# Stationary operands of the second attention product: even and odd columns in place of the two halves, and one product group in reverse order

## The chip, the cores and the metric

The kernel runs on one core of one Trainium2 chip. The metric is the device time of one execution in microseconds. The kernel before takes 2455.51 us, the median of three runs (2453.16 to 2455.78). The profile was taken of another execution, of 2453.05 us, whose instructions span 2451.3 us. TensorE (PE in the profile) was granted 0.999 of its full clock in it.

## What is computed

The reference is one self-attention layer on an input x of 4 images of 64 x 64 pixels with 256 channels, in float32:

```
q = einsum('bwhc,cd->bwhd', x, Wq) + bq        # 128 channels
k = einsum('bwhc,cd->bwhd', x, Wk) + bk        # 128 channels
v = einsum('bwhc,cd->bwhd', x, Wv) + bv        # 256 channels
pq, pk, pv = q.reshape(B, -1, N), k.reshape(B, -1, N), v.reshape(B, -1, N)   # N = 64 * 64
energy = einsum('bcn,bcm->bnm', pq, pk)
attention = softmax(energy, axis=-1)
out = einsum('bcm,bnm->bcn', pv, attention)
return gamma * out.reshape(x.shape) + x
```

For each of the 4 images this is an N x N = 4096 x 4096 matrix of energies, its softmax over m, and a product of that matrix with the 256 channels of v. The reshape is a reinterpretation of memory, so a row of pq is a run of pixels and channels and not one channel. The two large products dominate.

## The kernel before

**Tiling.** An image is worked through in 16 groups of 256 columns n (`NG`, index `g`), and a group in 8 steps of 512 rows m (`NU`, index `t`). With 4 images there are 4 x 16 x 8 = 512 steps, counted within an image by `u`. A step has two halves on TensorE:

- `energy` (L317 on) forms the energies of a later step (three ahead). It multiplies stationary blocks of k (128 x 128) with the moving operand q (128 x 256). Every operand is split into a high part, a low part and a correction, so that products in the fast format fp32r give full precision; a step has 12 such products (L330), eight into the tile `sa` and four into `sb`.
- `attend` (L363 on) multiplies the exponentials with v. The exponentials of the step are held in three tiles: `h` (high part), `l` (the rest) and `d` (a correction), each of 128 partitions x 4 blocks of m x 256 columns n. They are the stationary operands, 128 columns at a time. The moving operands are rows of `vh`, `vl` (258 wide: 256 channels and two columns of ones that give the sum of the softmax) and `vd` (256 wide).

A step has 3 parts (`h`, `l`, `d`) x 2 blocks of columns (`j`) x 4 blocks of m (`i`) = 24 products in `attend` (L380), so 36 with the energies. Every product needs a fresh stationary operand: each MATMUL has a weight load of its own, which the profile lists as LDWEIGHTS under the engine name PEld.

**Blocks of columns.** Block `j` of the stationary operand is `left[:, i, j*P:(j+1)*P]`: 128 neighbouring float32 values, 512 bytes, with a step of 4 bytes. The rows of the accumulators `acc[j]` and `bb[:, j, :]` are the columns n of that block.

**Places in memory.** All of this lies in SBUF. Rows of `vh` and `vl` are 260 values (1040 bytes) apart, those of `vd` 256 values (1024 bytes). Blocks `i` of `h`, `l` and `d` are 1024 bytes apart. `l` and `d` have two buffers each and `h` has three, each 4096 bytes. Small unused tiles (`pad`, `pad2`, `pad3`) set where the tiles start.

**Order.** The order of the work is written out by hand (`manual_schedule`); each engine runs its list in order. In a step TensorE does the 12 energy products of step u + 3 and then the 24 of `attend(u)`: the eight of `h`, the eight of `l`, the eight of `d`, and within a part j = 0 and then j = 1, each with i = 0 to 3. ScalarE (ACT) does the exponentials (L334) and `h` (L349), VectorE (DVE) the join of two exponentials (L344) and `l` and `d` (L355, L358). At the end of a group, `finish` (L400 on) scales the sums, transposes them back through TensorE into `tp` (L417), and adds them to the tile `xr` of the input (L421), which goes out by DMA. The last group of all has its own form, `finish_last`, with the addition at L465.

Of the kernel before, what the change touches and what calls it, by code (L numbers as in the profile page):

```python
# [13 lines left out]
ALU = mybir.AluOpType  # L14
# [6 lines left out]
def kernel(  # L21
# [36 lines left out]
    nc = tc.nc  # L58
    B, W, H, C = x.shape
    P = 128  # L60
# [115 lines left out]
    NJ = NB // P  # L176
# [24 lines left out]
    with ExitStack() as fast:  # L201
# [161 lines left out]
        def attend(b, u):  # L363

            g, t = divmod(u, NU)
            if t == 0:
                now["acc"] = [
                    ps_o.tile([P, C + 2], F32, tag=f"a{j}", name=f"a{j}_{b}_{g}")
                    for j in range(NJ)
                ]  # L370
                now["bb"] = ps_o.tile([P, NJ, C], F32, tag="bb", name=f"bb_{b}_{g}")
            h, l, d = units[b, u]
            acc, bb = now["acc"], now["bb"]
            for left, right in ((h, vh), (l, vl), (d, vd)):
                for j in range(NJ):
                    out_ = bb[:, j, :] if left is d else acc[j]
                    for i in range(4):
                        m = 2 * t + i // 2 + NI * (i % 2)

                        nc.tensor.matmul(  # L380
                            out_,
                            left[:, i, j * P : (j + 1) * P],
                            right[:, m, : out_.shape[1]],
                            start=(t == i == 0 and (left is h or left is d and j == 0)),
                            stop=(t == NU - 1 and i == 3 and left is not h),
                            skip_group_check=True,
                        )
            if t == NU - 1 and (b, g) != (B - 1, NG - 1):
                o = now["o"] = work.tile([P, NJ, C + 2], F32, tag="o", name=f"o_{b}_{g}")
                for j in range(NJ):  # L390
                    nc.scalar.activation(o[:, j, :], acc[j], AF.Identity, scale=1.0 + E)

        def factors(b, g, gamma):

            r = work.tile([P, 2, NJ], F32, tag="r", name=f"r_{b}_{g}")
            nc.vector.reciprocal(r[:, 0, :], zall[:, b * NG + g, :])
            nc.vector.tensor_tensor(r[:, 0, :], r[:, 0, :], gamma.to_broadcast([P, NJ]), ALU.mult)
            return r[:, 0, :], r[:, 1, :]

        def finish(b, g, o, bb, xr):  # L400
            yield
            yield

            nc.vector.tensor_copy(zall[:, b * NG + g, :], o[:, :, C])
            r, _ = factors(b, g, gam1)
            nc.vector.tensor_tensor(o[:, :, :C], o[:, :, :C], bb, ALU.add)
            yield
            for j in range(NJ):
                nc.scalar.activation(
                    o[:, j, :C], o[:, j, :C], AF.Identity, scale=r[:, j : j + 1]  # L410
                )
            yield
            yield
            tp = ps_t.tile([P, 2, NB], F32, tag="t", name=f"ot_{b}_{g}")
            for s in range(2):
                for j in range(NJ):
                    nc.tensor.transpose(  # L417
                        tp[:, s, j * P : (j + 1) * P], o[:, j, s * P : (s + 1) * P], ident
                    )
            yield  # L420
            nc.vector.tensor_tensor(xr, xr, tp, ALU.add)  # L421
            nc.gpsimd.dma_start(ov[b, g], xr)

        def guard():

            z = zall.rearrange("p n j -> p (n j)")
            ok = ppool.tile([P, 4, NB], F32, tag="y", name="ok")[:, 0, : B * NG * NJ]
            nc.vector.tensor_scalar(ok, z, Z_LOW, None, ALU.is_ge)
            nc.vector.scalar_tensor_tensor(ok, z, Z_HIGH, ok, ALU.is_le, ALU.mult)
            yield  # L430
            nc.vector.tensor_reduce(zs, ok, AX.X, ALU.min)
            nc.vector.tensor_scalar(zs, zs, 0.5, None, ALU.is_lt)
            zp = ps_s.tile([P, 1], F32, tag="b", name="zp")
            nc.tensor.matmul(zp, ones, zs, start=True, stop=True)
            yield
            nc.vector.tensor_copy(again, zp)
            yield
            yield

        def finish_last(b, g, xr):  # L440

            for j in range(NJ):
                a = now["acc"][j]
                nc.vector.tensor_copy(zall[:, b * NG + g, j : j + 1], a[:, C : C + 1])
            r, ra = factors(b, g, gam)
            check = guard()
            nc.vector.tensor_scalar(ra, r, 1.0 + E, None, ALU.mult)
            o = work.tile([P, NJ, C + 2], F32, tag="o", name=f"o_{b}_{g}")
            tps = []
            for j in range(NJ):  # L450
                next(check)
                nc.scalar.activation(
                    o[:, j, :C], now["bb"][:, j, :], AF.Identity, scale=r[:, j : j + 1]
                )
                nc.vector.scalar_tensor_tensor(
                    o[:, j, :C], now["acc"][j][:, :C], ra[:, j : j + 1], o[:, j, :C], ALU.mult, ALU.add
                )
                tp = (ps_t, ps_s)[j].tile([P, 2, P], F32, tag="ta"[j], name=f"ot_{b}_{g}_{j}")
                for s in range(2):
                    nc.tensor.transpose(tp[:, s, :], o[:, j, s * P : (s + 1) * P], ident)  # L460
                tps.append(tp)
            for j in range(NJ):
                next(check)
                n = slice(j * P, (j + 1) * P)
                nc.vector.tensor_tensor(xr[:, :, n], xr[:, :, n], tps[j], ALU.add)  # L465
            nc.sync.dma_start(ov[b, g], xr)

        def begin(b, i):
# [17 lines left out]
        for b in range(B):  # L486
# [20 lines left out]
            for u in range(STEPS):  # L507
                g, t = divmod(u, NU)
# [33 lines left out]
                for forms in beside:  # L542
                    next(forms)
                attend(b, u)
                if (b, u) == (B - 1, STEPS - 1):
                    finish_last(b, g, loads.pop((b, "x", g)))
                elif t == NU - 1:
                    start(finish(b, g, now["o"], now["bb"], loads.pop((b, "x", g))))
# [9 lines left out]
    NJ = NB // P  # L558
    NP = NM // 2
    xg, og = columns(x, NB), columns(out, NB)  # L560
    with tc.If(nc.values_load(again[0:1, 0:1]) > 0), ExitStack() as general:
# [8 lines left out]
        for b in range(B):  # L570
# [16 lines left out]
            for g in range(NG):  # L587
                ps = []
                mx = work.tile([P, 2, NB], F32, tag="mx", name=f"gmx_{b}_{g}")
                for t in range(NP):  # L590
# [9 lines left out]
                    p = ppool.tile([P, 2, NB], F32, tag="p", name=f"gp_{b}_{g}_{t}")  # L600
# [6 lines left out]
                tp = ps_t.tile([P, NJ, P], F32, tag="t", name=f"gmt_{b}_{g}")  # L607
# [40 lines left out]
                xr = xpool.tile([P, 2, NB], F32, tag="xr", name=f"gxr_{b}_{g}")  # L648
# [41 lines left out]
```

## Time and profile before

| Part | Busy, us | Share of the span |
|---|---|---|
| TensorE matmuls (PE) | 2438.7 | 99% |
| TensorE weight loads (PEld) | 2408.0 | 98% |
| VectorE (DVE) | 2099.0 | 86% |
| ScalarE (ACT) | 1795.2 | 73% |
| GpSimd (POOL) | 424.5 | 17% |

Matmuls overlap each other in these records: one of 256 columns is shown as some 280 ns long, while the next one starts some 115 ns after it. The busy share of PE therefore says only that there was always a matmul in flight. What counts is the **pitch**, the time from the start of one matmul to the start of the next. It is read from the timeline: a row there merges a run of equal instructions and has the start of the first one, so the difference of two starts, divided by the number of products between them, is their pitch.

The DMA queues moved 204 GB/s on average, with a mean busy share of the DMA engines of 0.6 to 0.7 in most of the span.

### The profile page before, as it was taken

Reading aid. Unit: us, or ns where it says so; the run is one execution under the profiler, and the core shown is the slowest. Engines: PE = TensorE matmul, PEld = TensorE weight load, DVE = VectorE, ACT = ScalarE, POOL = GpSimd, SP = SyncE. Lnnn points to the kernel's source line nnn. Section 1 sums busy time; section 2 is a strip of 40 time slices with the busy share of each in tenths; the row PEclk is TensorE's granted clock in tenths of the full one; section 3 lists DMA queues with packets and bytes.
Section 4 is the critical chain, followed back from the end, with each engine's and each line's share of the span. In section 5 each row is a group of like instructions: output and inputs, shape, how many; then the busy total and the mean of one; then the engine's idle time right before and its main releaser. Section 6 shows DMA issues by size and latency. Waiting matters only on the chain.

```text
span 2451.3 us, 50024 instructions
## 1 busy us (share of the span) xinstructions
PE 2438.7 (99%) x19982; PEld 2408.0 (98%) x19982; DVE 2099.0 (86%) x2314; ACT 1795.2 (73%) x3201; POOL 424.5 (17%) x781
## 2 busy tenths in 40 slices
PE   9999999999999999999999999999999999999998
PEld 8999999999899999999989999999998999999998
DVE  5988888888698888888869888888886988888887
ACT  5777777776677777777667777777766777777775
POOL 4211111111411111111141111111114111111110
PEclk9999999999999999999999999999999999999999
DMA  7766666665776666666477666666647766666663
GB/s 234 224 202 209 204 207 202 202 215 153 235 221 197 210 203 208 208 197 213 141 243 226 203 203 202 208 210 201 206 140 248 223 204 201 204 207 210 203 202 111
DMA packets 137407, 498.92 MB, mean 204 GB/s; under 512 B 15536, under 2 KB 57264, under 8 KB 137168
## 3 DMA queue, kind: packets, MB, share of 16 engines
q0 software_dynamic: 92320, 453.17, 60.0%
q1 hardware_dynamic: 44304, 42.22, 5.5%
q8 instruction: 160, 2.62, 0.4%
q14 instruction: 79, 0.65, 0.1%
q10 hardware_dynamic: 544, 0.26, 0.0%
HBM read 445.25 MB, written 50.33 MB: 202 GB/s over the span
## 4 chain that ended last, share of the span: by engine, by line


## 5 line engine op out<-in xcount | busy, mean ns | idle before, releaser
L334 ACT ACTIVATE x<-sa 128x512 f32<-128x512 f32 x1024 | 612.2, 598 | 516.1 <-PE sa L330 514.0
L344 DVE TENSOR_TENSOR x<-x,y 128x1024 f32<-128x1024 f32 x512 | 626.2, 1223 | 234.4 <-ACT y L334 234.4
L330 PE MATMUL sa<-q,k 128*128 128x256 f32 x4096 | 735.4, 279 | 0.0
L358 DVE SCALAR_TENSOR_TENSOR d<-h,x 128x1024 fp32r<-128x1024 f32 x512 | 623.3, 1217 | 0.0
L355 DVE TENSOR_TENSOR l<-x,h 128x1024 fp32r<-128x1024 f32 x512 | 623.2, 1217 | 0.0
L330 PEld LDWEIGHTS sa<-q,k 128*128 128x128 f32 x4096 | 619.4, 188 | 0.4
L334 ACT ACTIVATE y<-sb 128x512 f32<-128x512 f32 x1024 | 615.7, 601 | 0.0
L380 PE MATMUL a<-vh,h 128*128 128x258 f32 x4096 | 574.4, 283 | 0.0
L380 PE MATMUL a<-vl,l 128*128 128x258 f32 x4096 | 572.8, 282 | 0.0
L330 PE MATMUL sb<-q,k 128*128 128x256 f32 x2048 | 567.1, 277 | 0.0
L380 PE MATMUL bb<-vd,d 128*128 128x256 f32 x4096 | 558.6, 279 | 0.0
L314 POOL DMA_DIRECT2D k<-kf x512 | 279.1, 545 | 1573.3 <-PE sb L330 1548.3
L349 ACT ACTIVATE h<-x 128x1024 fp32r<-128x1024 f32 x512 | 543.8, 1062 | 8.3 <-DVE x L344 7.8
L380 PEld LDWEIGHTS a<-vl,l 128*128 128x128 f32 x4096 | 525.3, 189 | 0.0
L380 PEld LDWEIGHTS a<-vh,h 128*128 128x128 f32 x4096 | 522.9, 189 | 0.0
L380 PEld LDWEIGHTS bb<-vd,d 128*128 128x128 f32 x4096 | 515.1, 188 | 0.0
L330 PEld LDWEIGHTS sb<-q,k 128*128 128x128 f32 x2048 | 384.5, 188 | 0.1
L137 PE MATMUL qk<-wqk_sb,xts 128*128 128x256 f32 x512 | 121.0, 379 | 0.0
L158 PE MATMUL v<-xts,wv_sb 128*128 128x256 f32 x512 | 120.3, 379 | 0.0
L158 PEld LDWEIGHTS v<-xts,wv_sb 128*128 128x128 f32 x512 | 97.3, 190 | 13.2
L137 PEld LDWEIGHTS qk<-wqk_sb,xts 128*128 128x128 f32 x512 | 92.3, 190 | 10.0
L275 POOL DMA_DIRECT2D qd<-qks x128 | 69.2, 549 | 179.8 <-DVE qks L146 170.6
(56 smaller groups left out, 864.4 us busy)
## 6 DMA issues: line engine op xcount, KB each, us to landing
k<-kf POOLq DMA_DIRECT2D x512, 768.0 KB, 4.7
x<-in_x_dram SPq DMA_DIRECT2D x128, 256.0 KB, 3.9
kf<-f POOLq DMA_DIRECT2D x64, 384.0 KB, 4.0
out_dram<-x POOLq DMA_DIRECT2D x63, 256.0 KB, 2.5
qd<-qks POOLq DMA_DIRECT2D x128, 64.0 KB, 3.0
qr<-qd SPq DMA_DIRECT2D x64, 128.0 KB, 3.6
wv_sb<-in_L_conv_Wv_dram POOLq DMA_DIRECT2D x1, 256.0 KB, 5.7
out_dram<-x SPq DMA_DIRECT2D x1, 256.0 KB, 3.8
```

The lines of the kernel that those rows point to most:

```text
L137: nc.tensor.matmul(qk[:, s, :], self.xt[i][:, k, s, :], wqk_sb[:, k, :], start=(k == 0), stop=(k == KC - 1),)
L158: nc.tensor.matmul(vp[:, eh, :], wv_sb[:, k, eh * P : (eh + 1) * P], self.xt[i][:, k].rearrange("p s a -> p (s a)"), start=(k == 0), stop= ...
L275: nc.gpsimd.dma_start(qd[b, i // 2 + NG // 2 * s][:, i % 2, :], x[:, s, :C2])
L314: nc.gpsimd.dma_start(t.rearrange("p (i s) f d -> p i s (f d)", s=2), kf[b, u % NU])
L330: nc.tensor.matmul(to[:, i], kt[:, 2 * k + i, f, :], q[:, f], start=first, stop=last)
L334: nc.scalar.activation(to[:, 2 * k : 2 * k + 2, :], sp.rearrange("p i j d -> p i (j d)"), AF.Exp, scale=scale,)
L344: nc.vector.tensor_tensor(x, x, y, ALU.mult)
L349: nc.scalar.activation(h, units[b, u], AF.Identity, scale=UPPER)
L355: nc.vector.tensor_tensor(l, x, h.bitcast(F32), ALU.subtract)
L358: nc.vector.scalar_tensor_tensor(d, h.bitcast(F32), 1.0 + E, x, ALU.mult, ALU.subtract)
L380: nc.tensor.matmul(out_, left[:, i, j * P : (j + 1) * P], right[:, m, : out_.shape[1]], start=(t == i == 0 and (left is h or left is d and ...
```

## The change

Three edits, all of which concern the columns n of a group.

- Block `j` becomes every second column, `left[:, i, j::NJ]` with NJ = 2: j = 0 are the even columns, j = 1 the odd ones. A stationary operand is then 128 values with a step of 8 bytes, over 1024 bytes. Its purpose is that the weight load moves through memory by as many bytes in a given time as the stream of the moving operand does.
- In the part `l`, in the block j = 1 and in the steps t = 1 and t = 3 of each group, the four products over `i` are issued in reverse order. The sum is the same but for its order.
- The accumulators now hold even and odd columns, and so the final addition puts them back in place: `xr` is read and written with a step of two values. This is in `finish` (once for each group) and in `finish_last` (twice in all).

```diff
-                    for i in range(4):
+                    back = left is l and j == NJ - 1 and t in (1, 3)
+                    for i in reversed(range(4)) if back else range(4):
                         m = 2 * t + i // 2 + NI * (i % 2)
                         nc.tensor.matmul(
                             out_,
-                            left[:, i, j * P : (j + 1) * P],
+                            left[:, i, j::NJ],
                             right[:, m, : out_.shape[1]],
...
             yield
-            nc.vector.tensor_tensor(xr, xr, tp, ALU.add)
+            x = xr.rearrange("p s (n j) -> p s j n", j=NJ)
+            nc.vector.tensor_tensor(x, x, tp.rearrange("p s (j n) -> p s j n", j=NJ), ALU.add)
             nc.gpsimd.dma_start(ov[b, g], xr)
...
                 next(check)
-                n = slice(j * P, (j + 1) * P)
-                nc.vector.tensor_tensor(xr[:, :, n], xr[:, :, n], tps[j], ALU.add)
+                x = xr[:, :, j::NJ]
+                nc.vector.tensor_tensor(x, x, tps[j], ALU.add)
             nc.sync.dma_start(ov[b, g], xr)
```

The number of instructions on every engine, their order, and the addresses of all tiles stay as they were; only the four products named above change places among themselves.

## The prediction

> **What bounds the kernel now.** I read the busy table first, then the waits, then the timeline of TensorE in the steady part.
>
> ```profile
> PE 2438.7 (99%) x19982; PEld 2408.0 (98%) x19982; DVE 2099.0 (86%) x2314; ACT 1795.2 (73%) x3201; POOL 424.5 (17%) x781
> ```
>
> ```profile
> ACT x L334 <- PE sa L330: 514.0, 496, 1.7
> DVE x L344 <- ACT y L334: 234.4, 416, 0.7
> ```
>
> TensorE is in use 99% of the span; ScalarE waits 514 us for it, and VectorE 234 us for ScalarE. No wait of TensorE itself reaches 3 us in the list. So the end is set by how fast TensorE goes through its 19,982 products, and the pitch is the number to look for:
>
> ```profile
> 800.97 0.40 PE L330 MATMUL sa<-q,k 128*128 128x256 f32 x2
> ...
> 802.38 1.12 PE L380 MATMUL a<-vh,h 128*128 128x258 f32 x8
> 803.34 1.12 PE L380 MATMUL a<-vl,l 128*128 128x258 f32 x8
> 804.29 1.09 PE L380 MATMUL bb<-vd,d 128*128 128x256 f32 x8
> 805.23 0.39 PE L330 MATMUL sa<-q,k 128*128 128x256 f32 x2
> ...
> 806.59 1.12 PE L380 MATMUL a<-vh,h 128*128 128x258 f32 x8
> 807.54 1.11 PE L380 MATMUL a<-vl,l 128*128 128x258 f32 x8
> 808.50 1.09 PE L380 MATMUL bb<-vd,d 128*128 128x256 f32 x8
> 809.42 0.39 PE L330 MATMUL sa<-q,k 128*128 128x256 f32 x2
> ```
>
> The first column is the start in us. The 12 energies take 802.38 - 800.97 = 1.41 us in the first step, a pitch of 117.5 ns, and 806.59 - 805.23 = 1.36 us in the second, 113.3 ns: the same instructions on the same shapes. The eights of h and l take 0.95 to 0.96 us (119 to 120 ns), those of d 0.94 and 0.92 us (117 and 115 ns).
>
> Over the whole trace, start to start: products of attend have a pitch between 112 and 125 ns, and none that waits for nothing goes below 112. The values repeat to about 1 ns in every group of every image for the same t, part, j and i, so they are tied to addresses and order and not to chance or to other engines. The fastest, 113.3 ns, occurs with 256 columns (d) and with 258 (for instance h, t = 2, j = 0, i = 2). I take **113.3 ns as the floor** of a product with a weight load. Above it lie, with stretches over 128 ns (true waits) left out: 26.6 us in h, 25.2 in l, 11.2 in d and 4.7 in the energies, **67.7 us in all**.
>
> **What the Trainium skill says.**
> - "TensorE: Matmul & The Clock Gate", section "LDWEIGHTS (loading the stationary operand)": a load takes the number of columns over 1.2 GHz, 128 / 1.2 = 106.7 ns. Its section "Back-to-back issue gap" gives N / 2.4 + 2.5 ns for a matmul: 109.2 ns for 256 columns, 110.0 for 258. The trace's floor of 113.3 lies above both and is the same for both widths, so the load with some 7 ns beside it seems to set it. Then anything that lengthens a load lengthens the pitch at once.
> - "SBUF — State Buffer", section "Who interferes with whom": TensorE has two read ports, one for the moving operand and one for weight loads, independent, and never waits on anyone. The trace doesn't agree fully: pitches differ by up to 12 ns with the addresses of the two operands alone, so the two reads disturb each other somewhere.
> - The same page, section "Specifications (TRN2)": memory lines of 16 bytes, with at least two hits on a line needed for full bandwidth. A step of 8 bytes gives two float32 values to a line, just enough. No strided stationary operand exists in this trace to compare.
>
> **The change part by part.**
>
> 1. *Step of 8 bytes, 12,288 products of attend.* In one pitch the moving stream goes through 1024 or 1032 bytes and the load through 512. Their distance slides by some 512 bytes within each product, and whatever makes them collide is met several times. With a step of 8 the load also covers 1024 bytes in the same time, so their distance stays put: they either collide once, shift against each other and run free, or keep out of each other's way from the start. Bounds: at best all of h, l and d at the floor, 26.6 + 25.2 + 11.2 = 63.0 us saved. At worst each load touches twice as many lines and meets twice as many collisions, 63.0 us lost. I take the first direction, since the trace has a regime of it: in d (rows and blocks both a multiple of 1024 bytes apart, so a constant distance from product to product) j = 1 runs at 113.3 to 113.6 ns throughout in t = 0, 2, 4, 5, 6 and 7, after a first four that cost 14.1, 11.4, 23.4, 23.4, 9.5 and 13.3 ns in sum above the floor. Over all t these first four cost 16.7 ns on average; I read that as settling. A step enters a new pair of tiles three times (h, l, d). If each entry keeps such a cost, 3 x 16.7 ns x 512 = 25.6 us remain; if none does, 0. I take the middle, 12.8 us.
>
> 2. *Four products of l in reverse, t = 1 and 3.* Exactly after t = 1 and t = 3 the trace shows d (j = 1) at 117.5 to 122.9 ns and the energies that follow at 117.5; after the other six they run at 113.3, with the same tiles. The mode is handed on from d to the energies (in 68 steps of 436 that could be read both are slow, in 368 both fast, none mixed). A reversed l enters d from another row, which can end this. The instructions are the same in number. Bounds: 0 and the 4.7 us of the energies; their part of d is in item 1. I take 4.7, since item 1 alone could already break the mode.
>
> 3. *Additions with a step (L421, 63 times, 680 ns each).* If the stride doubled them, VectorE would be busy 43 us longer. It lies beside TensorE: in 1000 to 1100 us VectorE is busy 88.0 of 100. The output DMA behind it on GpSimd's queue waits for it 211.9 us in all without anyone waiting for that output; the tile goes back to the loads of x, which are asked for two steps ahead. The loads of k in the same queue (L314) are ahead of need by 3.7 us of waiting each. Cost 0. The built order shows DVE's loads and these outputs with one more wait each, on a load that landed steps before: 0.
>
> 4. *The last addition (L465, twice 418 ns).* It is on the path, after the last product. Between 0 and 0.8 us; I take 0.4, which is lost in rounding.
>
> Does something else become the bound? At 67.7 - 12.8 = 54.9 us less (2.2%) VectorE goes to some 90 of 100 in the same stretch and ScalarE from 75.2 to 77. Neither reaches TensorE. k moves 768 KB a step, 4.7 us from issue to landing, with two steps (8.2 us) until it is needed.
>
> Sum: 2455.5 - 63.0 - 4.7 + 12.8 + 0.4 = **2401 us**.
>
> **The rivals.**
> - *Half.* Streams at equal speed collide for a whole product where the distance is wrong, and rows of vh and vl (1040 bytes apart) bring a new distance each time. Then some products gain and others lose; with half the excess left, 2455.5 - 34 = 2421 us, from 2413 to 2450. For it: h and l have a wide spread of pitches, 113 to 125. Against: a collision shifts the two, after which equal speeds no longer meet.
> - *No change.* The spread comes from how the moving rows lie (their lines begin at other places), not from the step: 2455 us. Against: d, with aligned rows, shows the same spread in its first four.
> - *Slower.* The load is the floor, and a step of 8 takes twice the lines. With twice the collisions 2455.5 + 63 = 2518 us; if a load needed one more cycle of 1.2 GHz for each of its 64 further pairs of values, 53 ns x 12,288 = 655 us more, 3110. For it: the floor is the load's, and the trace has no strided load. Against: two hits to a line should still be full speed.
>
> **How the numbers follow.** The forecast (2385 to 2413) has a chance of 0.51, half 0.23, no change 0.05, slower 0.21. The first three together are 0.79; the range goes from 2385, just below all of 67.7 us saved (2388), to 2462, which takes in no change and the mildest of slower. Within 0.2% of before is 2450.6 to 2460.4: 0.06 with the edges. Faster 0.73, slower 0.21.
>
> **What would show it.** In the profile after: eights of h, l and d that start 0.91 to 0.92 us apart, twelve energies in 1.36 us in every step, among them after t = 1 and 3; a step of 4.08 to 4.13 us in place of 4.19 to 4.26; LDWEIGHTS of 188 ns as now. L421 up to twice 680 ns would hurt nothing. I am wrong if L380's loads grow longer than 192 ns or the eights take more than 0.96 us; and item 2 is wrong if the energies after t = 1 and 3 stay at 1.41 us.

## The result, and the profile after

The changed kernel takes 2488.3 us (median of four runs, 2486.9 to 2489.8), the kernel before 2454.3 us beside it. The ratio is 1.0138, with a 95% interval of 1.0121 to 1.0156: **slower by 34 us**, where 2401 was forecast.

The busy table of the page after:

```profile
PE 2472.8 (100%) x19982; PEld 2442.0 (98%) x19982; DVE 2099.4 (84%) x2314; ACT 1795.4 (72%) x3201; POOL 424.5 (17%) x781
```

TensorE is longer busy by 34.1 us (2472.8 for 2438.7), by just what the run is longer; VectorE and ScalarE do the same work as before. So nothing new became the bound. The list of waits says the same from the other side: ScalarE still waits for TensorE (514.0 us before) and VectorE for ScalarE (234.4).

```profile
ACT x L334 <- PE sa L330: 472.1, 435, 1.7
DVE x L344 <- ACT y L334: 267.0, 420, 0.8
ACT x L334 <- DVE x L344: 72.7, 58, 1.3
```

The third row is new: in 58 of its waits ScalarE is now released last by VectorE. TensorE doesn't wait for it; no wait of TensorE in the list is longer than 2.4 us in all, as before.

The timeline of TensorE, first column the start in us. A row with x8 is one run of eight products of a part, called an eight from here on:

```profile
808.37 1.13 PE L383 MATMUL a<-vh,h 128*128 128x258 f32 x8
809.34 1.14 PE L383 MATMUL a<-vl,l 128*128 128x258 f32 x8
810.31 1.12 PE L383 MATMUL bb<-vd,d 128*128 128x256 f32 x8
811.27 0.39 PE L330 MATMUL sa<-q,k 128*128 128x256 f32 x2
```

The eights of h and l start 0.97 us apart (121 ns a product), that of d takes 0.96 (120 ns). Before they took 0.95 to 0.96 and 0.92 to 0.94. The loads of these products before:

```profile
L380 PEld LDWEIGHTS a<-vl,l 128*128 128x128 f32 x4096 | 525.3, 189 | 0.0
L380 PEld LDWEIGHTS a<-vh,h 128*128 128x128 f32 x4096 | 522.9, 189 | 0.0
L380 PEld LDWEIGHTS bb<-vd,d 128*128 128x128 f32 x4096 | 515.1, 188 | 0.0
```

and after, with a group of the energies below them:

```profile
L383 PEld LDWEIGHTS a<-vl,l 128*128 128x128 f32 x4096 | 536.3, 197 | 0.0
L383 PEld LDWEIGHTS a<-vh,h 128*128 128x128 f32 x4096 | 534.1, 196 | 0.0
L383 PEld LDWEIGHTS bb<-vd,d 128*128 128x128 f32 x4096 | 533.3, 196 | 0.0
L330 PEld LDWEIGHTS sb<-q,k 128*128 128x128 f32 x2048 | 384.6, 188 | 0.1
```

The last number ahead of the second bar is the mean length of one load: 196 to 197 ns with the step of 8 bytes, 188 to 189 before, and still 188 in the energies, whose operands did not change. (Loads overlap each other in these records, as matmuls do, so this length isn't the pitch.) Of the mean pitches over the whole trace (pitches over 130 ns, true waits, left out), h goes from 119.8 to 121.7 ns, l from 119.5 to 121.6, d from 116.1 to 120.4. Times 4096 each that is 7.8 + 8.8 + 17.8 = **34.4 us: the whole of the difference lies in these three rows**, and half of it in d, which was the best off before.

### The profile page after: what moved, and what is told of

The parts are those of the page before. It is cut to its first block, busy times and chain, and to the rows that moved or that the text cites. A ratio compares the mean times of both kernels' runs of the same rounds, so it can differ in the third digit from the quotient of the medians.

```text
span 2485.1 us, 50092 instructions
## 1 busy us (share of the span) xinstructions
PE 2472.8 (100%) x19982; PEld 2442.0 (98%) x19982; DVE 2099.4 (84%) x2314; ACT 1795.4 (72%) x3201; POOL 424.5 (17%) x781
## 4 chain that ended last, share of the span: by engine, by line
## 5 line engine op out<-in xcount | busy, mean ns | idle before, releaser
L383 PE MATMUL a<-vh,h 128*128 128x258 f32 x4096 | 582.3, 285 | 0.0
L383 PE MATMUL a<-vl,l 128*128 128x258 f32 x4096 | 581.2, 285 | 0.0
L383 PE MATMUL bb<-vd,d 128*128 128x256 f32 x4096 | 576.0, 283 | 0.0
L383 PEld LDWEIGHTS a<-vl,l 128*128 128x128 f32 x4096 | 536.3, 197 | 0.0
L383 PEld LDWEIGHTS a<-vh,h 128*128 128x128 f32 x4096 | 534.1, 196 | 0.0
L383 PEld LDWEIGHTS bb<-vd,d 128*128 128x128 f32 x4096 | 533.3, 196 | 0.0
L158 PE MATMUL v<-xts,wv_sb 128*128 128x256 f32 x512 | 120.3, 379 | 0.0
```

The costliest lines, as they stand in the source:

```text
L158: nc.tensor.matmul(vp[:, eh, :], wv_sb[:, k, eh * P : (eh + 1) * P], self.xt[i][:, k].rearrange("p s a -> p (s a)"), start=(k == 0), stop= ...
L383: nc.tensor.matmul(out_, left[:, i, j::NJ], right[:, m, : out_.shape[1]], start=(t == i == 0 and (left is h or left is d and j == 0)), sto ...
```

## The experiments

**The two edits apart.** First the changed kernel without the reversed order.

```diff
-                    for i in reversed(range(4)) if back else range(4):
+                    for i in range(4):
```

> The changed kernel without the reversed order of l. Theory A (the step of 8 bytes is the whole cause: +34 us, and the reversal is a small repair of one bad hand-over): 2490 us, that is 2488 or up to 5 us more, with the pitch of h, l and d at 120 to 122 ns as in the changed kernel, and the energies after t = 3 at some 117 ns instead of 113.3. Theory B (the reversal puts the streams out of step and costs a good part of the 34 us): 2455 to 2475 us.

Measured: 2490.0 us, ratio to before 1.0145 (1.0129 to 1.0160). The step alone costs all of it. The pitches are 121.8, 121.6 and 120.3 ns. The energies after t = 3 run at 113.6 ns and not at the 117 that was expected: the step itself breaks the slow mode (the pitch of 117.8 ns that these energies had before), so the reversal had little left to mend here, and by time the two runs with a step can't be told apart.

Then the reversal without the step:

```diff
-                    for i in range(4):
+                    back = left is l and j == NJ - 1 and t in (1, 3)
+                    for i in reversed(range(4)) if back else range(4):
```

> The kernel before with the four products of l in reverse order in t = 1 and 3, and blocks of neighbouring columns as before. Theory A: within 5 us of before (2454), in either direction, since the order alone adds no access; if it ends the slow mode after t = 1 and 3 with this step too, 2 to 5 us less. Theory B: 10 to 34 us more than before.

Measured: 2450.4 us, ratio 0.9979 (0.9971 to 0.9987), **5.1 us faster than before**. With neighbouring columns, d (j = 1) in t = 3 falls from 117.5 to 113.3 ns, and so do the energies after it (from 117.8). In t = 1, d falls to 113.3 ns in three of its four products of j = 1, but that brought nothing: in 60 of 64 groups four transposes come between this d and the next energies, and the last six of those twelve energies went from some 113.6 ns up to 115.4 and more. Summed over the trace, the excess over 113.3 ns of the products of t = 1 and of the energies after them is 9.6 us before and after. All of the gain lies in t = 3. Theory A holds in both runs: step and reversal are two changes with opposite signs.

**Is it the load, or the two reads meeting?** The moving operand is held still: all 258 or 256 columns are the same value of the row, so that the moving stream stays at one place in memory while the number of columns is as before. The edit is made to both kernels.

```diff
-                            right[:, m, : out_.shape[1]],
+                            right[:, m, C - (left is d) :][:, :1].to_broadcast([P, out_.shape[1]]),
```

> The changed kernel with the moving operand of attend held still: each product reads one value of its row (in h and l the one of the column of ones) again and again, 258 or 256 times, so that the moving stream goes through no memory. The sums are others for that. Theory C (the two reads collide): the pitch of h, l and d falls to the floor of 113 to 114 ns, 2488 - 97 = some 2390 us. Theory D (a load with a step of 8 bytes takes longer by itself): the pitch stays at 120 to 122 ns, 2480 to 2490 us, and the loads stay at 196 ns.

> The kernel before with the moving operand of attend held still in the same way. Theory C: the pitch of h, l and d falls from 116 to 120 to 113 to 114 ns, 2454 - 63 - 4 = some 2388 us, the same as with the step of 8 bytes. Theory D: the same here, since the load of neighbouring values is not longer; the two theories part in the run with the step.

Measured: 2459.7 us with the step, 2386.5 us with neighbouring columns, one execution each. Timeline of TensorE with the step and a still operand:

```profile
801.78 1.10 PE L383 MATMUL a<-vh,h 128*128 128x258 f32 x8
802.71 1.11 PE L383 MATMUL a<-vl,l 128*128 128x258 f32 x8
803.66 1.10 PE L383 MATMUL bb<-vd,d 128*128 128x256 f32 x8
804.60 0.40 PE L330 MATMUL sa<-q,k 128*128 128x256 f32 x2
```

and with neighbouring columns and a still operand:

```profile
803.21 1.05 PE L380 MATMUL a<-vh,h 128*128 128x258 f32 x8
804.10 1.06 PE L380 MATMUL a<-vl,l 128*128 128x258 f32 x8
804.99 1.06 PE L380 MATMUL bb<-vd,d 128*128 128x256 f32 x8
805.88 0.38 PE L417 MATMUL ot<-ident,o 128*128 128x128 f32 x2
```

In the second every eight takes 0.89 us: in the whole trace these products have a pitch of 111 to 112 ns, whatever t, part, j and i (the first of a step apart). The spread between 112 and 125 ns is gone, so it needs a moving operand that goes through memory. In the first the eights take 0.93 to 0.95 us, 117 to 118 ns nearly everywhere. Neither theory C (113 to 114 ns) nor theory D (120 to 122) fits by itself; each has a part: with a still operand both kernels lose their spread, and 6 ns remain that belong to the step. (In both runs the energies after `attend` are mostly slow, at 114.6 to 118 ns; they are left out of the reading.)

**The load by itself, and steps of other widths.** A still operand reads one place again and again, and the load could have met that place. So the stream is cut short instead: in t = 1 to 7 only the last 34 columns (32 in d) are multiplied. If the pitch stays where a still operand had it, the load alone sets it (the bare load). The edit, here in the changed kernel, is made to the kernel before as well.

```diff
-                            out_,
+                            out_ if t == 0 else out_[:, 224:],
                             left[:, i, j::NJ],
-                            right[:, m, : out_.shape[1]],
+                            right[:, m, 224 * (t > 0) : out_.shape[1]],
```

> The changed kernel with a moving operand of attend of 34 columns (the last ones) instead of 258 or 256 in all steps but t = 0; most of the sums are left out for that. [...] Theory D (a load with a step of 8 bytes takes some 6 ns longer by itself): 117 to 118 ns for t = 1 to 7. Theory E (in the run with the step and a still operand the load was held up by the one place that is read again and again, which a load over 1024 bytes passes twice as often): 112 to 114 ns, as with neighbouring values.

> The kernel before with the same moving operands of 34 columns; most of the sums are left out. Both theories: a pitch of 107 to 113 ns for t = 1 to 7, the bare load of 128 neighbouring values. If it were far below that, the load would not set the floor, and both would fall.

In both runs the granted clock of TensorE fell to half of full speed for long stretches (means of 0.67 and 0.71), and the times, 3485.7 and 3271.2 us, say nothing about the load; pitches are read where the clock was full. With neighbouring columns, in such a stretch, its row of the windows first (the number 1.00 behind POOL is the granted clock), then its timeline:

```profile
177.50:179.50 2.00, 2.00 (x20) 2.00 (x20) 1.98 (x5) 1.96 (x4) 0.58 (x2) 1.00 0.94 180
```

```profile
177.58 1.04 PE L380 MATMUL a<-vl,l 128*128 128x34 f32 x8
178.48 1.04 PE L380 MATMUL bb<-vd,d 128*128 128x32 f32 x8
```

and with the step of 8 bytes:

```profile
955.40:957.40 2.00, 2.00 (x19) 2.00 (x19) 2.00 (x3) 2.00 (x4) 0.13 (x1) 1.00 0.83 229
```

```profile
955.40 1.10 PE L383 MATMUL a<-vl,l 128*128 128x34 f32 x8
956.34 1.09 PE L383 MATMUL bb<-vd,d 128*128 128x32 f32 x8
957.28 0.49 PE L330 MATMUL sa<-q,k 128*128 128x256 f32 x2
```

0.90 us against 0.94. Over all stretches at full clock: 111.7 ns against **118.0 ns** (l). A product of 34 columns takes as long as one of 258 with a still operand (111.7 and 111.7 with neighbouring columns, 118.0 and 117.8 with the step): the load sets the pitch, and with a step of 8 bytes the load itself takes 6.3 ns longer. Theory E is out.

Two more steps say what a load pays for. Only the stationary operand differs from the run with 8 bytes; 16 bytes:

```diff
-                            left[:, i, j::NJ],
+                            left.rearrange("p i n -> p (i n)")[:, 512 * (i // 2) + 2 * (i % 2) + j : 512 * (i // 2) + 512 : 4],
```

> As the run with the step of 8 bytes and 34 columns, but a step of 16 bytes: 128 values out of 512, so one value on each line of 16 bytes (the blocks take other columns and rows for that, and the sums are others). Theory D, if lines count: four times the lines of neighbouring values, where a step of 8 has twice; the excess of some 6 ns becomes 18 to 20 ns (a pitch of 130), or more, since a line has one hit only. Theory D, if any step costs a fixed time: 117 to 118 ns again. Theory E: 112 to 114 ns.

and 12 bytes:

```diff
-                            left[:, i, j::NJ],
+                            left.rearrange("p i n -> p (i n)")[:, 160 * i + j : 160 * i + 384 : 3],
```

> As the runs with a moving operand of 34 columns, with a step of 12 bytes: 128 values out of 382, on 96 lines of 16 bytes (the blocks take other columns for that, and the sums are others). Theory F (a load pays for lines: 233.5 ns / 128 lines = 1.82 ns each, and takes the longer of this and 111.7 ns): 64 lines give 117 ns for the step of 8, as measured (118.0), and 96 lines 175 ns here. Theory G (a threshold: under two hits on a line the load falls to half speed as a whole): 230 to 236 ns, as with 16 bytes. Theory H (a small fixed cost of any step up to some width): 118 ns.

Measured at full clock, 16 bytes, its windows row and timeline:

```profile
84.30:86.00 1.70, 1.70 (x9) 1.70 (x9) 1.07 (x3) 1.23 (x3) 0.00 (x0) 1.00 0.87 249
```

```profile
84.33 2.02 PE L383 MATMUL a<-vl,l 128*128 128x34 f32 x8
86.20 2.03 PE L383 MATMUL bb<-vd,d 128*128 128x32 f32 x8
```

and 12 bytes:

```profile
808.70:810.10 1.40, 1.40 (x10) 1.40 (x10) 0.31 (x1) 1.06 (x3) 0.00 (x0) 1.00 0.79 118
```

```profile
808.66 1.55 PE L383 MATMUL a<-vl,l 128*128 128x34 f32 x8
810.07 1.55 PE L383 MATMUL bb<-vd,d 128*128 128x32 f32 x8
```

1.87 us for eight loads with 16 bytes, 1.41 us with 12. (The times of the two runs, 4407.0 and 3824.0 us, again have stretches at half clock in them, with means of 0.64 and 0.73.) The means over the trace, for l (the last column where the clock was half):

| Step, bytes | Lines of 16 bytes for 128 values | Pitch, ns | Lines x 1.82 ns | Pitch at half clock, ns |
|---|---|---|---|---|
| 4 | 32 | 111.7 | 58 | 213.3 |
| 8 | 64 | 118.0 | 117 | 213.3 |
| 12 | 96 | 175.3 | 175 | 213.3 |
| 16 | 128 | 233.4 | 233 (sets the 1.82) | 233.3 |

The 12 bytes were forecast at 175 from the 16 bytes alone. **At full clock a load takes the longer of two times: its 128 values, 111.7 ns, or its lines of 16 bytes, 1.82 ns each** (theory F). At 8 bytes the lines have just overtaken the values (the rule gives 117 there, 1.3 ns less than measured). A threshold (230 ns and more at 12 bytes) and a fixed cost (118) are both out. The first expectation of 130 ns for 16 bytes was far too low, since it scaled the excess and not the lines.

The stretches at half clock bear the rule out a second time. There the time for the values grows to 213.3 ns and covers steps of 4, 8 and 12 bytes; with 16 bytes the pitch stays at 233.3, so in these runs the time for the lines doesn't follow the clock of TensorE. The run with 16 bytes at half clock (0.50 behind POOL), eights 1.87 us apart as at full clock:

```profile
100.70:104.30 3.60, 3.60 (x17) 3.60 (x16) 2.45 (x2) 0.49 (x2) 0.00 (x0) 0.50 0.67 212
```

```profile
100.63 2.03 PE L383 MATMUL a<-vl,l 128*128 128x34 f32 x8
102.50 2.03 PE L383 MATMUL bb<-vd,d 128*128 128x32 f32 x8
```

One thing stays open. In all four runs the number of lines is the span of the operand in bytes divided by 16, so a price for each line and a price for each byte of the span (0.114 ns) give the same numbers. A step of 32 bytes, with as many lines as 16 and twice the span, would part the two; it was not run.

**One part alone.**

```diff
-                            left[:, i, j * P : (j + 1) * P],
+                            left[:, i, j::NJ] if left is d else left[:, i, j * P : (j + 1) * P],
```

> The kernel before with the step of 8 bytes in the part d alone, neighbouring values in h and l (the sums mix columns for that). If the cost belongs to each strided load by itself (4096 of the 12,288), d rises from 116.1 to some 120.4 ns as in the changed kernel, and the time by some 4096 x 4.3 ns = 18 us to 2473; h and l stay at 119 to 120 ns. If the cost came from all three parts working against each other, d alone would stay near 116 ns and the time under 2460 us.

Measured: 2472.5 us, ratio 1.0067 (1.0052 to 1.0082). d has 120.4 ns, h and l stay at 119.8 and 119.6. The strided loads of d bring their cost with neighbouring values in h and l too, so it isn't the three parts working against each other.

**The reversal further.** With neighbouring columns, first in every t (the line that differs from the reversal above):

```diff
+                    back = left is l and j == NJ - 1
```

> Blocks of neighbouring columns, and the four products of l, j = 1, in reverse order in every step t instead of in 1 and 3 alone. If the reversal is good as such: below the run with t = 1 and 3 (2450 us), 2440 to 2447. If it only happens to end a bad hand-over after t = 1 and 3, the other steps get as often worse as better: 2448 to 2460.

Measured: 2450.9 us, ratio 0.9983 (0.9975 to 0.9992), as with t = 1 and 3. By step, the sum of the excesses over 113.3 ns in a step's products, over the whole trace, went down in t = 3, 4 and 5 (12.3 to 6.8 us, 7.7 to 6.8, 7.7 to 6.9) and up in t = 2, 6 and 7; in t = 0 and 1 it hardly moved. So only those three were kept:

```diff
+                    back = left is l and j == NJ - 1 and t in (3, 4, 5)
```

> Neighbouring columns, with the four products of l, j = 1, in reverse order in t = 3, 4 and 5, the steps in which the two runs with the reversal had a lower sum of pitches (h, l, d and the energies after) than the kernel before: 12.3 to 6.8 us in t = 3, 7.7 to 6.8 in t = 4, 7.7 to 6.9 in t = 5. If the steps add up independently: 7.2 us less than before, 2448 us. If a change in one step is handed on to the next, 2449 to 2455.

Measured: **2448.7 us, ratio 0.9971 (0.9960 to 0.9983)**, below both kernels of this case. Its timeline shows the eight of d in t = 3 at 0.92 us, and the twelve energies after it, from 801.84 to 803.20, at 1.36 us; the same twelve took 1.41 us before (from 800.97 to 802.38):

```profile
800.92 1.08 PE L381 MATMUL bb<-vd,d 128*128 128x256 f32 x8
801.84 0.39 PE L330 MATMUL sa<-q,k 128*128 128x256 f32 x2
...
803.20 1.12 PE L381 MATMUL a<-vh,h 128*128 128x258 f32 x8
```

The mean of d is 115.3 ns (116.1 before). The gain is 7.2 us, as expected for steps that add up as if each were alone.

## Why the prediction was wrong

**What bounds the kernel** was right: TensorE by its pitch, and the pitch by the load. The two runs with 34 columns show it directly. The floor was 1.6 ns too high: 113.3 ns is the best with a moving stream, 111.7 the bare load. One comparison of the prediction was looser than it reads: the Trainium skill, in "TensorE: Matmul & The Clock Gate", section "Back-to-back issue gap", gives N / 2.4 + 2.5 ns for a matmul in isolation, and says that in a stream of loads and matmuls both set the spacing. In these runs the load does, at 111.7 ns for 34 columns and for 258 with a still operand.

**Item 1 failed, and with it the forecast: the term that was left out is the load's own time.** The item counted only collisions, and took the floor as the same with a step, from what the Trainium skill says in "SBUF — State Buffer", section "Specifications (TRN2)": two hits on a line for full bandwidth. The same row goes on that each cross to a new line pays a penalty, which the item didn't use. For a weight load, two hits are not quite enough by the measurement, which decides: 118.0 ns against 111.7, and 12,288 x 6.3 ns = **77 us more**. The prediction had said itself that anything that lengthens a load lengthens the pitch at once, and then did not put a price on it.

A gain of about the size that the item counted was there. Above the bare load lay, before, 119.8 - 111.7 = 8.1 ns in h, 7.8 in l and 4.4 in d; after, above 118.0, 3.7, 3.6 and 2.4. Times 4096 that is 18 + 17 + 8 = 43 us saved, where the item had 63.0 - 12.8 = 50. 77 - 43 = 34 us, the measured loss; this is one difference of pitches split in two, not a second measurement of it.

That the excess falls because the two streams now move at equal speed, the item's mechanism, is not shown, and one run speaks for another reason. With a step of 12 bytes the step t = 0 still has its full moving operand, and its load spans 1536 bytes beside 1032 of the stream, so the speeds differ. Yet at full clock its eights of l and d start 1.41 us apart, as with 34 columns:

```profile
803.20:805.90 2.70, 2.70 (x17) 2.70 (x17) 2.37 (x2) 1.06 (x3) 0.00 (x0) 1.00 0.92 282
```

```profile
803.15 1.57 PE L383 MATMUL a<-vl,l 128*128 128x258 f32 x8
804.56 1.57 PE L383 MATMUL bb<-vd,d 128*128 128x256 f32 x8
```

Over the trace the full stream adds some 0.4 to 1.5 ns to the load there, less than at 8 bytes (2.4 to 3.7) or at 4 (4.4 to 8.1). So a longer load by itself seems to leave room for the stream, and that 43 us came near to 50 is no proof of equal speeds; as far as these runs go it may be luck.

**Item 2** had the mechanism right for t = 3 and the sum too large. The reversal alone ends the slow mode after t = 3 and brings 5.1 us, but of the 4.7 us that the item counts in the energies only 2.4 came (their mean goes from 114.1 to 113.7 ns); the rest came from d and l, and t = 1 gave nothing. In the changed kernel the mode was already gone by the step, as the item had feared, but other energies became slower (after t = 2 from 113.3 to 114.0 ns, for instance), so that the mean of all is 114.0 and only 0.4 of the 4.7 us came. The order there is worth 1.7 us between medians whose intervals overlap.

**Items 3 and 4** were right, with nothing to pay at all: the addition L421, now L425, has 680 ns as before, and the two at the end 418. So these additions are no slower with a step of 8 bytes. The added waits that the item mentions, 63 instructions on GpSimd and 5 on SyncE, show no cost either: the outputs wait 211.8 us for L425 where they waited 211.9.

**The rivals.** "Slower" named the cause, a load that sets the floor and twice the lines, and then priced it wrongly at both ends: by twice the collisions (63 us) and by one cycle for each pair of values (655 us). The bare load costs 77 us, and the collisions did not double but halved. "Half" and "no change" did not occur.

What was to show the forecast wrong did: loads longer than 192 ns (196 to 197), and eights over 0.96 us (0.97). The trace before had no strided load, so the price could not be read there; to lean on "just enough" where the load has no slack at all was the wrong choice.

## What to carry to other kernels

Where every matmul needs a fresh stationary operand, read the pitch from the starts in the timeline and ask what a bare load takes: cutting the moving operand short, at full clock, measures it. A strided stationary operand cost 1.82 ns for each 16 bytes that it spans here, against 0.87 ns for each value, whichever sum is longer; of the four steps measured with float32, only neighbouring values kept clear of the first. A gain that is real (43 us of excess) doesn't help if it is bought by lengthening the one operation that has no slack (77 us).

## What the runs showed of the hardware that was not expected

- A load of 128 float32 values takes 111.7, 118.0, 175.3 and 233.4 ns with steps of 4, 8, 12 and 16 bytes at full clock, and 213.3, 213.3, 213.3 and 233.3 ns at half clock.
- A moving stream through memory lengthens the pitch: with it held still, h and l fall from 119.8 and 119.5 ns to some 111.6 each. Whether the load waits for the stream or the stream for the load, and in which places of memory the two meet, stays open; the lengths of the load records don't tell (188 to 189 ns with the stream, 190 to 192 with a still operand).
- Two pitches are possible for the same instructions on the same tiles (energies after t = 3 at 113.3 or 117.8 ns), and which it is comes from the products before; the order of four products decides it for twelve others.
- The kernel before with products of 34 columns in t = 1 to 7, and a load for every one as before, was granted half its clock for much of the span (mean 0.71), where the same loads with 258 columns kept the full clock (0.999).
